# A graph network kernel on one core: the layouts of two more pairs turned by transfers

## The chip, the cores and the metric

The kernel runs on one core of one Trainium2 chip. The metric is the device time of one execution in microseconds (us), of which the median of three runs is given. A profile of one execution shows where the time goes.

## The reference

The input is 64 graphs of 256 nodes with 256 features each, and an adjacency matrix for each graph. Two layers follow one another. The first is a gated graph network of three steps; the second is an attention over neighbours. Each is added to its input and normalised.

```python
def gnn(x, adj, weight, w_ih, w_hh, b_ih, b_hh):
    A = (adj != 0).astype(x.dtype)
    h = x
    for i in range(3):
        m = einsum('bnd,de->bne', h, weight[i])
        aggr = einsum('bst,bsd->btd', A, m)
        h = gru_cell(aggr, h, w_ih, w_hh, b_ih, b_hh)   # r, z: sigmoid; n: tanh
    return h                                             # h = (1 - z) * n + z * h

def gat(h, adj, W, a):
    Wh = h @ W
    e = leaky_relu((Wh @ a1)[:, :, None] + (Wh @ a2)[:, None, :], 0.2)
    attn = softmax(where(adj > 0, e, NEG_INF), axis=2)
    return attn @ Wh

x = layernorm(x + gnn(x, adj, ...))
x = layernorm(x + gat(x, adj, W, a))
```

## The kernel before

Two graphs make a pair, and there are 32 pairs, numbered 0 to 31. One gated step of one pair is a block, written (p, i) for pair p and step i. Blocks run in turns: turn t holds the blocks (t, 0), (t-1, 1) and (t-2, 2), so that three pairs are always under way. The attention of a pair is spread over the two turns after its last step.

The order of all instructions is written out by hand. The function `gates` issues the matrix products of a block (line 468, three pieces of each operand to keep float32 accuracy) and calls `tick` at fixed places in them, 12 ticks in a block. Every other step of the kernel is put on a list with the tick at which it is due (`at`, `after`) and is issued when the clock gets there. Each engine then works through its own instructions in the order of issue. All transfers of the middle of the kernel go out on one queue, that of SyncE (SP).

The work needs two layouts. The products take h with features on the partitions (`hT`). The aggregation over neighbours (`aggregate`, line 439) takes x or h with nodes on the partitions, as two pieces `hi` and `lo` in float32r. So x must be turned once for each pair, and h must be turned back before step 1 and before step 2. There are two ways to do it, and the constant `FROM` tells which pair takes which.

Pairs below `FROM` are turned on TensorE. `to_T` (line 280) turns x with eight 128x128 transposes into PSUM, and an evacuation on ScalarE or VectorE writes `hT`. `from_T` (line 369) turns h with eight transposes before each of the steps 1 and 2; `split` (line 405) and `rest` (line 135) make hi and lo from PSUM. x is loaded (`load_x`) 7 ticks and adj (`load_adj`) 5 ticks after the step before has begun its preparation.

Pairs from `FROM` on are turned by transfers. The transfers that transpose move 16-bit halves, so a float32 value comes out as two planes that must be put together again. `x_turned` (line 347) issues one transposing transfer of x from DRAM into `first`, four copies (line 357) sort the halves into `second`, and `x_joined` writes `hT` with 16-bit copies on ScalarE and VectorE (`put_together`, line 289). For h, `h_turned` issues two transposing transfers from `hT` into `first_h` (line 299) and four copies into `second_h` (line 305); then `join` makes `V` (line 289), `split` makes hi on ScalarE (line 329) and `rest` makes lo on VectorE (line 135). `first` shares the single buffer of x, and `second` and `second_h` share the single buffer of adj, so x and adj of such a pair are loaded only after them, 33 and 34 ticks after the preparation of the block before has begun.

```python
FROM = L + 2
...
nxt = np_ + 1
if nxt < FROM:
    after(7, lambda p=nxt: load_x(p))
elif nxt < NP:
    later = {}
    after(26, lambda p=nxt, d=later: d.update(f=x_turned(p)))
    after(30, lambda d=later: d["f"]())
    after(33, lambda p=nxt: x_joined(p))
    after(33, lambda p=nxt: load_x(p))
after(5 if nxt < FROM else 34, lambda p=nxt: load_adj(p))
```

The ticks at which a block's own steps are due are called its pace. A first step below `FROM` takes the pace `EARLY`; from `FROM` on it takes `FIRST`. Other names that occur below: `ones` (line 380) makes the 0/1 matrix `A` from adj on VectorE; hH, hL and hD are the three pieces of hT (lines 132, 135 and 138, on ScalarE, GpSimd and VectorE), and aH, aL, aD those of the aggregate.

Of the kernel before, what the change touches and what calls it, by code (L numbers as in the profile page):

```python
# [27 lines left out]
def kernel(  # L28
# [39 lines left out]
    L = weight.shape[0]  # L68
# [24 lines left out]
    def after(dt, step):  # L93
        at(clock[0] + dt, step)
# [67 lines left out]
    neg = const.tile([P, 1], F32, name="neg")  # L162

    loaded, loaded_adj = {}, {}
    FROM = L + 2

    def load_x(p):
        if p < NP:
            x_sb = loaded[p] = io.tile([P, G, C, D], F32, tag="x", name=f"x_{p}")
            nc.sync.dma_start(x_sb, x[p * G:(p + 1) * G].rearrange("g (c p) d -> p g c d", p=P))  # L170

    def load_adj(p):
        if p < NP:
            a_sb = loaded_adj[p] = io.tile([P, G, C, N], I32, tag="adj", name=f"adj_{p}")
            nc.sync.dma_start(a_sb, adj[p * G:(p + 1) * G].rearrange("g (c p) n -> p g c n", p=P))
# [100 lines left out]
    def to_T(src, dst, d):  # L276

        pt = bank("pt")
        for k in range(K):
            nc.tensor.transpose(pt[:, k * P:(k + 1) * P], src[:, k // C, k % C, d * P:(d + 1) * P], ident)  # L280
        after(1, lambda: evacuate(dst[:, d, :], pt))
# [25 lines left out]
    def h_turned(p, i, e):  # L307

        s = pairs[p]
        pool, dt = ((late, (16, 19, 22)), (io, (12, 22, 25)))[i]  # L310
        tmp = {}

        def first():
            tmp["a"] = first_of(pool.tile([P, G, C, D], F32, tag=("wh", "x")[i], name=f"first_h{p}_{i}"))
            for d in range(C):
                turn_half(tmp["a"], s.hT, d)

        def second():
            tmp["b"] = second_of(io.tile([P, G, C, D], F32, tag="adj", name=f"second_h{p}_{i}"))
            gather(tmp["b"], tmp["a"])  # L320

        def join(d):
            tmp[d] = work.tile([P, K, P], F32, tag="V", name=f"V{d}_{p}_{i}", bufs=1)
            put_together(tmp[d].rearrange("p k n -> p (k n)"),
                         *(tmp["b"][:, h, :, d * P:(d + 1) * P] for h in (1, 0)), "av" if i == 0 else "va", k=K)

        def split(d):
            s.hi[d] = work.tile([P, K, P], F32R, tag=f"hi{d}", name=f"hi{d}_{p}_{i + 1}", bufs=1)
            nc.scalar.copy(s.hi[d], tmp[d])

        def rest(d):
            s.lo[d] = work.tile([P, K, P], F32R, tag=f"lo{d}", name=f"lo{d}_{p}_{i + 1}", bufs=1)
            lower(nc.vector, s.lo[d], tmp[d], s.hi[d])
        s.hi, s.lo = [None] * C, [None] * C
        at(e + dt[0], first)
        at(e + dt[1], second)
        for d in range(C):
            for n, step in enumerate((join, split, rest)):
                at(e + dt[2] + (2, 4)[i] * d + n, lambda step=step, d=d: step(d))
        s.by_dma = i + 1  # L340
# [31 lines left out]
    def begin(p):  # L372
        s = pairs.setdefault(p, Pair())
        s.hT = work.tile([P, C, GN], F32, tag="hT", name=f"hT_{p}", bufs=4)
# [10 lines left out]
    def front(p, i, t, pace):  # L385
# [7 lines left out]
        def turn(d):  # L393
            s = pairs[p]
            if i == 0:
                if p < FROM:
                    to_T(s.x, s.hT, d)
# [491 lines left out]
    for n, (p, i) in enumerate(blocks):  # L889
        if n + 1 < len(blocks):  # L890
            np_, ni = blocks[n + 1]
            if ni == 0:
                if np_ < FROM:
                    after(1, lambda p=np_: begin(p))
                after(1, lambda p=np_: take_x(p))
                after(2, lambda p=np_: ones(p))
# [4 lines that stand above are left out]
# [4 lines left out]
                    after(33, lambda p=nxt: load_x(p))  # L905
                after(5 if nxt < FROM else 34, lambda p=nxt: load_adj(p))
            front(np_, ni, clock[0], 
                  CLOSE if n and np_ == blocks[n - 1][0] else
                  EARLY if np_ < FROM and not ni else (FIRST, SECOND, THIRD)[ni])
        gates(p, i, (2, 3, 5) if n + 2 >= len(blocks) or blocks[n + 2][0] == p else (2, 5, 9))  # L910
        if i == L - 1:
            if p < NP - len(LAST):
                attention(p, clock[0])
            else:
                attention_last(p, clock[0], LAST[p - NP])
        elif FROM <= p and p + i + 1 < NP:
            h_turned(p, i, clock[0])
# [32 lines left out]
```

## Time and profile before

| | before |
|---|---|
| median of three runs | 2091.16 us (2088.38 to 2096.8) |
| time of the profiled execution | 2091.86 us |
| its span, first to last instruction | 2090.0 us |
| granted TensorE clock | 0.996 |
| packets' bytes moved by DMA | 247.98 MB |

The profile gives each engine's busy time; PE is TensorE's matmuls, PEld its weight loads, DVE is VectorE, ACT ScalarE and POOL GpSimd. A line of a timeline has the start in us, the duration in us, the engine, the kernel's line, the operation, what is written and read, and in brackets how long the engine was idle before it and what ended that. A line of the waits names the engine and line that waited, whom it waited for, the sum in us, how often, and the longest.

### The profile page before, as it was taken

What the parts mean: (1) busy time and instruction counts of PE and PEld (TensorE: products, weight loads), DVE (VectorE), ACT (ScalarE), POOL (GpSimd) and SP (SyncE); (2) the same over time, 40 slices, a digit from 0 to 9 for tenths busy, and PEclk for the clock granted to TensorE, in tenths of its full rate; (3) what the DMA queues carried; (4) which work ended last, traced back from release to release, by engine and by line L of the source; (5) the groups of instructions that cost most, each with busy time, mean ns of one, the idle gap of its engine ahead of it and who ended that gap; (6) DMA issues with size and microseconds to landing.
All of it is one profiled execution on the core that took longest, in us unless ns stands there. A gap on an engine that the chain in (4) does not pass through costs nothing.

```text
span 2090.0 us, 31381 instructions
## 1 busy us (share of the span) xinstructions
PE 2052.3 (98%) x9892; PEld 1726.0 (83%) x9892; DVE 1780.5 (85%) x2886; ACT 1655.3 (79%) x3015; POOL 1604.8 (77%) x1114
## 2 busy tenths in 40 slices
PE   8999999999999999999999999999999999999996
PEld 5788888888888888888888888888888888888885
DVE  5666778898888899888998988998888998988887
ACT  4566787888887888888888887888888888888775
POOL 6777777777877787878777877787878787878763
PEclk9999999999999999999999999999999999999998
DMA  4111235665666665665665666665766665666321
GB/s 131 31 41 41 72 88 114 141 141 117 136 138 135 141 137 121 136 136 137 140 136 124 136 137 137 137 138 123 134 138 139 134 141 123 138 136 137 61 61 61
DMA packets 531621, 247.98 MB, mean 119 GB/s; under 512 B 359616, under 2 KB 523200, under 8 KB 531456
## 3 DMA queue, kind: packets, MB, share of 16 engines
q1 hardware_dynamic: 529664, 244.14, 53.1%
q8 instruction: 79, 1.29, 0.3%
q10 hardware_dynamic: 1616, 1.57, 0.2%
q14 instruction: 86, 0.70, 0.1%
q0 software_dynamic: 176, 0.27, 0.1%
HBM read 69.74 MB, written 33.55 MB: 49 GB/s over the span
## 4 chain that ended last, share of the span: by engine, by line
PE 89%; DVE 3%; ACT 3%; issue 2%; POOL 1%; DMA 1%; SPq 0%; POOLq 0%; ACTq 0%; DVEq 0%
PE pga L468 46%; PE pgb L468 23%; PE pa L439 8%; PE pwh L589 5%; PE po L673 5%; DVE lo L135 1%; PE s L608 1%; PE pt L369 1%; ACT sc L636 1%; DMA rows_hH<-in_L_gnn_w_hh_dram 0%; PE po L796 0%; ACT L636 0%; PE pw L238 0%; ACT n L475 0%; DMA second<-v 0%
## 5 line engine op out<-in xcount | busy, mean ns | idle before, releaser
L494 POOL TENSOR_TENSOR t<-hT,n 128x512 f32<-128x512 f32 x192 | 263.0, 1370 | 191.6 <-ACT n L486 191.3
L500 POOL TENSOR_TENSOR n<-n,r 128x512 f32<-128x512 f32 x192 | 316.5, 1648 | 81.8 <-ACT r L486 42.6
L504 POOL TENSOR_TENSOR n<-n,t 128x512 f32<-128x512 f32 x192 | 282.7, 1472 | 122.7 <-DVE t L477 116.0
L468 PE MATMUL pga<-hH,whhH_whh 128*128 128x512 f32 x1152 | 370.5, 403 | 0.0
L468 PE MATMUL pgb<-hD,whhD_whh 128*128 128x512 f32 x1152 | 356.8, 391 | 1.4 <-DVE hD L138 1.4
L468 PE MATMUL pga<-hL,whhL_whh 128*128 128x512 f32 x1152 | 356.7, 391 | 0.4 <-POOL hL L135 0.4
L495 POOL TENSOR_TENSOR t<-t,z 128x512 f32<-128x512 f32 x192 | 271.4, 1414 | 15.1
L135 POOL TENSOR_TENSOR hL<-hT,hH 128x1024 fp32r<-128x1024 f32 x96 | 255.5, 2661 | 9.0 <-ACT hH L132 9.0
L468 PEld LDWEIGHTS pgb<-hD,whhD_whh 128*128 128x128 f32 x1152 | 216.2, 188 | 49.2 <-DVE hD L138 1.7
L468 PEld LDWEIGHTS pga<-hL,whhL_whh 128*128 128x128 f32 x1152 | 216.2, 188 | 47.8 <-POOL hL L135 0.8
L468 PEld LDWEIGHTS pga<-hH,whhH_whh 128*128 128x128 f32 x1152 | 207.5, 188 | 34.1
L473 ACT ACTIVATE r<-pga 128x512 f32<-128x512 f32 x192 | 114.1, 594 | 109.1 <-PE pga L468 79.6
L439 PE MATMUL pa<-A,lo 128*128 128x256 f32 x768 | 192.5, 283 | 6.1 <-DVE lo L135 6.1
L138 DVE SCALAR_TENSOR_TENSOR hD<-hH,hT 128x1024 fp32r<-128x1024 f32 x96 | 195.7, 2039 | 0.0
L439 PE MATMUL pa<-A,hi 128*128 128x256 f32 x768 | 194.2, 285 | 0.2 <-DVE A L380 0.2
L477 DVE SCALAR_TENSOR_TENSOR r<-pgb,r 128x512 f32<-128x512 f32 x192 | 132.0, 687 | 68.9 <-PE pgb L468 43.4
L486 ACT ACTIVATE n<-n,bi 128x512 f32<-128x512 f32 x192 | 139.1, 724 | 64.0 <-POOL n L504 63.8
L507 DVE TENSOR_TENSOR hT<-t,n 128x512 f32<-128x512 f32 x192 | 185.0, 963 | 0.0
L135 DVE TENSOR_TENSOR aL<-pa,aH 128x512 fp32r<-128x512 f32 x192 | 130.9, 682 | 56.6 <-ACT aH L132 56.5
L473 ACT ACTIVATE t<-pga 128x512 f32<-128x512 f32 x192 | 115.1, 600 | 71.1 <-PE pga L468 66.0
L132 ACT ACTIVATE aH<-pa 128x512 fp32r<-128x512 f32 x192 | 115.8, 604 | 64.0 <-PE pa L439 64.0
L439 PEld LDWEIGHTS pa<-A,lo 128*128 128x128 f32 x768 | 146.4, 191 | 13.8 <-DVE lo L135 7.6
(172 smaller groups left out, 5405.9 us busy)
## 6 DMA issues: line engine op xcount, KB each, us to landing
adj<-in_adj_dram SPq DMA_DIRECT2D x64, 512.0 KB, 3.8
second_h<-first_h SPq DMA_DIRECT2D x204, 128.0 KB, 4.2
x<-in_x_dram SPq DMA_DIRECT2D x32, 512.0 KB, 3.8
xT<-hT SPq DMA_DIRECT2D x32, 512.0 KB, 4.5
vT<-xT SPq DMA_DIRECT2D x32, 512.0 KB, 3.3
second<-v SPq DMA_DIRECT2D x116, 128.0 KB, 3.8
sc<-eT SPq DMA_DIRECT2D x232, 64.0 KB, 2.3
out_dram<-eT SPq DMA_DIRECT2D x29, 512.0 KB, 4.3
```

What stands on the lines that cost most here:

```text
L135: eng.tensor_sub(dst, src, hi.bitcast(F32))
L138: nc.vector.scalar_tensor_tensor(dst, hi.bitcast(F32), 1.0 + U, src, op0=ALU.mult, op1=ALU.subtract)
L439: nc.tensor.matmul(pt[:, g * N:(g + 1) * N], h[:, g * C + c, :], s.A[:, g, c, :], start=(n == 0), stop=(n == len(todo) - 1))
L468: nc.tensor.matmul(pt, w[:, d, o * P:(o + 1) * P], m[:, d, :], start=n in (0, ends + 1), stop=n in (ends, len(todo) - 1))
L473: nc.scalar.activation(dst, a, AF.Copy, scale=1.0 + U)
L477: nc.vector.scalar_tensor_tensor(dst, b, -1.0 / U, dst, op0=ALU.mult, op1=ALU.add)
L486: nc.scalar.activation(dst, dst, func, bias=bias)
L494: nc.gpsimd.tensor_sub(t, h, n)
L495: nc.gpsimd.tensor_mul(t, t, z)
L500: after(2, lambda r=r, n=n: nc.gpsimd.tensor_mul(n, n, r))
L504: after(1, lambda n=n, t=t: nc.gpsimd.tensor_add(n, n, t))
L507: after(lags[2], lambda n=n, t=t, h=h: nc.vector.tensor_add(h, t, n))
```

## The change

`L` is 3, the number of steps. `FROM` goes from 5 to 3, so that pairs 3 and 4 are turned by transfers too. Pairs 0, 1 and 2 stay on TensorE.

```diff
-    FROM = L + 2
+    FROM = L
```

All that depends on `FROM` follows for these two pairs: the transposes and evacuations of `to_T` and `from_T` are not issued; `x_turned`, `x_joined` and `h_turned` are; x and adj are loaded at ticks 33 and 34 instead of 7 and 5; and the first step's pace is `FIRST` instead of `EARLY`.

```python
EARLY = (2, 1, 2, 6, 7, 8), (5, 8, 10)
FIRST = (2, 1, 2, 7, 7, 8), (3, 10, 7)
```

The numbers are the ticks of turn, split, rest, aggregate and the two pieces of the aggregate, and then of hH, hL and hD.

## The prediction

> **What bounds the kernel now.** I read the page first, for the engine that is never idle:
>
> ```profile
> PE 2052.3 (98%) x9892; PEld 1726.0 (83%) x9892; DVE 1780.5 (85%) x2886; ACT 1655.3 (79%) x3015; POOL 1604.8 (77%) x1114
> PE 89%; DVE 3%; ACT 3%; issue 2%; POOL 1%; DMA 1%; SPq 0%; POOLq 0%; ACTq 0%; DVEq 0%
> ```
>
> PE is busy for 98% of the span and holds 89% of the chain that ended last. Second, the longest of PE's own waits:
>
> ```profile
> PE pa L439 <- DVE lo L135: 6.1, 5, 1.2
> ```
>
> Outside the start and the tail this is the only wait that costs PE more than 2 us: five times 1.2 us in 2090. So the middle of the kernel is a stream of matmuls in a fixed order, and what leaves the stream is saved unless something new interrupts it. Third, the timeline of PE around two groups of transposes says what they take from it:
>
> ```profile
> 141.74 0.62 PE L468 MATMUL pgb<-aD,wc2D_wc 128*128 128x512 f32 x2
> 142.19 0.60 PE L280 MATMUL pt<-ident,x 128*128 128x128 f32 x4
> 142.55 0.70 PE L468 MATMUL pga<-hH,whhH_whh 128*128 128x512 f32 x2
> 143.09 0.63 PE L468 MATMUL pga<-hL,whhL_whh 128*128 128x512 f32 x2
> 143.56 0.62 PE L468 MATMUL pgb<-hD,whhD_whh 128*128 128x512 f32 x2
> 144.01 0.60 PE L280 MATMUL pt<-ident,x 128*128 128x128 f32 x4
> ```
>
> Starts matter here, since neighbours overlap. A pair of 128x512 matmuls takes about 0.455 us from start to start. From 142.19 to 144.01 there are 1.82 us, with three such pairs (1.36) and four transposes in them: a group of four costs 0.46 us, 0.115 each, although one lasts 272 ns. Fourth, the table of stretches, cut at the first matmul of each block. Here are blocks (1,2), (2,2), (5,0), (7,0), (4,1), (6,1); the first two columns are the length and PE's busy time:
>
> ```profile
> core 0: us, PE busy (x) PEld busy (x) DVE busy (x) ACT busy (x) POOL busy (x), PEclk, DMA share, GB/s
> 197.20:216.40 19.20, 19.20 (x97) 16.20 (x96) 11.83 (x19) 14.50 (x25) 14.91 (x10) 1.00 0.17 55
> 262.40:280.70 18.30, 18.30 (x90) 15.43 (x89) 16.13 (x32) 14.02 (x24) 16.70 (x12) 1.00 0.46 115
> 280.70:303.90 23.20, 23.20 (x118) 19.60 (x117) 16.23 (x27) 18.81 (x39) 15.60 (x14) 1.00 0.13 46
> 408.20:430.50 22.30, 22.30 (x109) 18.83 (x108) 17.91 (x34) 19.73 (x41) 16.40 (x14) 1.00 0.34 95
> 303.90:326.60 22.70, 22.70 (x113) 19.23 (x112) 17.48 (x28) 17.34 (x31) 16.18 (x10) 1.00 0.58 140
> 430.50:452.30 21.80, 21.80 (x105) 18.47 (x104) 20.09 (x27) 18.76 (x33) 16.73 (x10) 1.00 0.63 132
> ```
>
> The rows come in couples: the same kind of block with eight transposes, then without. The differences are 0.9 us each, PE is full in both, and ACT, DVE and DMA carry more in the second and still do not stop it. This is the change, already run on later pairs.
>
> **What the Trainium skill says.** "Perfetto Trace Analysis", section "Identifying the Most-Contended Engine", says that pipelined matmuls make busy time a poor measure of PE; agreed, which is why I price by starts: 272 ns by its record against 0.115 us. "TensorE: Matmul & The Clock Gate", section "Part 4: PE-mode transpose", puts a transpose in a kernel at about 275 ns; the record agrees (272), the cost to a full PE does not. "DMA: Bandwidth & Descriptors", section "DMA Transpose (X-bar)", says that such a transfer moves 2-byte types only and lands in SBUF; that is why the code turns 16-bit halves and joins them afterwards. "SBUF — State Buffer", section "SBUF: two separate sides", says that a DVE operation with two SBUF inputs and a GpSimd one that reads SBUF exclude each other for a whole instruction. The trace agrees, on one pair of instructions, in blocks (9,1) and (10,1):
>
> ```profile
> 628.00 2.93 DVE L135 TENSOR_TENSOR lo<-V,hi 128x512 fp32r<-128x512 f32 x1
> 628.00 2.38 POOL L135 TENSOR_TENSOR hL<-hT,hH 128x1024 fp32r<-128x1024 f32 x1
> 630.99 0.39 PE L439 MATMUL pa<-A,lo 128*128 128x256 f32 x1 [1.22 <-DVE lo L135]
> ...
> 691.85 0.68 DVE L135 TENSOR_TENSOR lo<-V,hi 128x512 fp32r<-128x512 f32 x1
> 691.85 2.94 POOL L135 TENSOR_TENSOR hL<-hT,hH 128x1024 fp32r<-128x1024 f32 x1
> ```
>
> Both start together. When DVE goes first nothing is lost; when POOL goes first, lo takes 2.93 us instead of 0.68 and PE waits. That is all five waits above; the block is 23.27 us long instead of 21.79, so a lost draw costs 1.48 us. It is lost 5 times in 25 turns.
>
> **The change part by part.**
> Removed from PE: per pair 8 transposes of x (L280) and 8 of h for each of two layers (L369), 24; 48 for two pairs, in six blocks of eight. By starts 48 x 0.115 = 5.5 us. By blocks: x in (0,2) and (1,2), 19.24 to 18.30, 0.94 each; h in (4,0) and (5,0), 23.21 to 22.29, 0.92 each; h in (4,1), 22.73 to 21.79, 0.94; h in (5,1), 22.75 to 21.79, 0.96. Sum 5.62. I take 5.6 us off; PE is full on both sides, so it lies on the path.
> ACT and DVE: per pair ACT loses 5 evacuations of 0.58 (2.9) and gains 2 joins of 0.77, 4 V copies of 0.77 and 4 hi of 0.61 (7.1): +4.2. DVE loses 5 of 0.68 (3.4) and gains 2 of about 0.7, 4 V of 0.87 and 4 lo of 0.72 (7.8): +4.4. Taken at nothing: blocks (7,0) and (6,1) above hold this load at ACT 19.73 and DVE 20.09 with PE full. The cover ends where a block has more than PE's length of it; without cover the cost would be at most the sum for two pairs, about 9 us.
> Order of the join of pair 3. It comes before aH and aL of (0,2). aD ended at 137.7 and PE takes it at 141.74. Two joins on ACT (1.4) and two on DVE (1.3) add at most 2.7: ready by 140.4. Nothing.
> SP. Per pair one DRAM transpose (4.6 us to landing), four copies into second (3.1), and twice two transposes (3.7) and four copies (4.2): 17 issues, 34 in all, on the one queue that also carries x, adj, xT, vT and the attention's eT. x and adj of pairs 3 and 4 move behind first, second and, for adj, the join. For pair 3 the join ends near 135 us; adj then needs 0.4 to issue and 3.8 to land, 139.2; ones(3) ran on DVE at 140.45. Margin about 1 us there and 8 us at PE (the aggregate starts at 148.58). No attention uses the queue yet. In the later turns the same chain leaves x and adj 4.4 and 2.9 us early (x issued 696.47, hi at 704.73; adj issued 700.94, A at 707.49). Between 0 and one landing (3.8 us) per pair, 0 to 8 in all; I take 0. A gain is excluded, since PE does not wait for x or adj there.
> Pace. Pair 3 and 4 take FIRST for EARLY: the aggregates one tick later, hL two ticks later, hD three earlier. PE's count is unchanged and the later turns run it; nothing.
> New draws. The blocks (4,1) and (5,1) get the lo and hL that start together: 2 x 5/25 x 1.48 = +0.6. The other 25 are drawn anew.
>
> Sum for the profiled execution: 2090.0 - 5.6 + 0.6 = 2085.0 of span, plus the 1.86 around it: 2086.9 against its 2091.86. Its time lies 0.7 above the median shown, so the median goes from 2091.16 to 2086.2, -0.24%. A measurement of this kernel can tell about 0.5% (10.5 us) from no change, and the three runs spread over 8.4 us, so by that measure this is "the same".
>
> **Rivals.**
> A, all draws lost. The transfers shift the turn so that POOL goes first each time: 27 lost for 5, 22 x 1.48 = 32.6, less 5.6: 2118. For it: the two start within 10 ns. Against: it won 20 of 25, and the late turns lost none. It ends slower than before from 4 more losses, slower by 0.5% from 11 more. One or two more is likely, eleven is not.
> B, all draws won. 5 x 1.48 = 7.4 on top: 2078. For it: the last seven turns are clean. It takes four fewer losses to pass 0.5%.
> C, late adj. SP's queue in turns 3 and 4 delivers late and DVE stands at ones, with the gates' evacuations queued behind it: +3.8 per pair, 2093. Against: the same chain is early in a fuller queue.
> D, hidden transposes. If another engine set these blocks, nothing would change: 2091. Against: the couples of blocks above, 0.9 us apart.
> E, full price. If a transpose cost its 272 ns, 13 us: 2078. Against: the starts.
>
> **How the numbers follow.** The forecast, with losses within three of five: 0.81, 2082 to 2091. B, with four or more fewer: 0.06. A: 0.05, of which 0.02 beyond 0.5%. C 0.05, a fifth of it beyond 0.5% if it hits more turns; D 0.02; E 0.01. Leaving out the far ends gives 2080.5 to 2091.5. Faster by over 0.5%: B and E, 0.07. Slower: 0.03. Same: 0.90.
>
> **What would show it.** Blocks (0,2) and (1,2) at 18.3, (4,0) and (5,0) at 22.3, (4,1) and (5,1) at 21.8, and L280 at 24 and L369 at 72 of hT instead of 40 and 104. Wrong would be: a PE wait on A, hi or aL between 120 and 410 us; those blocks still 0.9 longer; or a count of 2.9 us long lo far from five.

## The result and the profile after

The changed kernel takes 2080.35 us (2078.74 to 2080.64, four runs) against 2093.18 (2088.38 to 2096.8) of the kernel before in the same comparison: a ratio of 0.9934, 95% interval 0.9919 to 0.9949. That is 12.8 us or 0.66% faster, clear of noise, and 2.6 times the forecast of 5.0 us. 2080.35 lies just below the range given.

The head of the page and the chain that ended last:

```profile
span 2078.6 us, 31369 instructions
PE 2048.2 (99%) x9844; PEld 1724.7 (83%) x9844; DVE 1787.8 (86%) x2896; ACT 1659.6 (80%) x3025; POOL 1616.4 (78%) x1114
PE 96%; DVE 1%; POOL 1%; ACT 1%; DMA 0%; issue 0%; POOLq 0%; ACTq 0%; SPq 0%; DVEq 0%
```

PE has 48 matmuls fewer, ACT and DVE ten instructions more each, and the chain is now PE for 96% of the span instead of 89%. The transposes that are left, by line (duration least, median, most):

```profile
L280 PE MATMUL pt<-ident,x x24: 270/347/448, 6.0 to 89.1; 128*128 128x128 f32 x24
L369 PE MATMUL pt<-ident,hT x72: 270/272/421, 70.8 to 2000.3; 128*128 128x128 f32 x72
```

The six blocks that lost transposes, in the table of stretches: (0,2), (1,2), (4,0), (5,0), (4,1), (5,1). Length first, then PE's busy time:

```profile
142.00:160.30 18.30, 18.30 (x90) 15.45 (x89) 13.54 (x19) 11.57 (x20) 16.88 (x11) 1.00 0.51 141
198.70:217.00 18.30, 18.30 (x89) 15.43 (x88) 15.13 (x22) 14.16 (x25) 16.88 (x11) 1.00 0.79 167
217.00:239.30 22.30, 22.30 (x110) 18.84 (x109) 19.21 (x33) 17.79 (x37) 16.36 (x14) 1.00 0.16 47
280.30:302.60 22.30, 22.30 (x109) 18.83 (x108) 18.15 (x35) 20.01 (x42) 16.94 (x14) 1.00 0.33 95
302.60:324.40 21.80, 21.80 (x106) 18.47 (x104) 20.09 (x27) 18.76 (x33) 16.74 (x10) 1.00 0.55 130
365.00:386.70 21.70, 21.70 (x105) 18.43 (x104) 20.00 (x27) 18.65 (x33) 16.65 (x10) 1.00 0.58 130
```

They are as long as their later counterparts, and PE is full in each. From block start to block start they are 5.7 us shorter in sum than before. PE's own waits, the four longest (sum, times, longest):

```profile
PE pt L280 <- DMA x<-in_x_dram: 6.0, 1, 6.0
PE pt L784 <- ACT sc L772: 4.4, 7, 1.4
PE pt L369 <- DVE vT L707: 3.1, 1, 3.1
PE pw L247 <- ACT gwT L229: 2.3, 1, 2.3
```

Every wait of PE of more than 0.1 us now lies in the first 70 us or in the tail. The line of `pa` waiting for `lo` (6.1 us, five times) is gone altogether: all 27 draws between lo and hL were won. Block (9,1), one of the five that had lost:

```profile
624.84 0.68 DVE L135 TENSOR_TENSOR lo<-V,hi 128x512 fp32r<-128x512 f32 x1
624.84 2.94 POOL L135 TENSOR_TENSOR hL<-hT,hH 128x1024 fp32r<-128x1024 f32 x1
```

The two profiles differ by 11.4 us of span. Block by block: -5.7 in the six blocks, five times -1.48 (-7.4) in the blocks of the lost draws, -0.5 in (24,0), where one `pwh` no longer waits, -0.5 in the tail, and +2.5 in the start-up, whose instructions are unchanged: block (0,0) starts at 23.0 instead of 21.8 and is 32.4 long instead of 31.1. The start differs that way between other kernels below too, so it is not put down to the change.

### The profile page after: what moved, and what is told of

Read it like the earlier page. It is cut to its first block, busy times and chain, and to the rows that moved or that the text cites. A ratio compares the mean times of both kernels' runs of the same rounds, so it can differ in the third digit from the quotient of the medians.

```text
span 2078.6 us, 31369 instructions
## 1 busy us (share of the span) xinstructions
PE 2048.2 (99%) x9844; PEld 1724.7 (83%) x9844; DVE 1787.8 (86%) x2896; ACT 1659.6 (80%) x3025; POOL 1616.4 (78%) x1114
## 4 chain that ended last, share of the span: by engine, by line
PE 96%; DVE 1%; POOL 1%; ACT 1%; DMA 0%; issue 0%; POOLq 0%; ACTq 0%; SPq 0%; DVEq 0%
PE pga L468 50%; PE pgb L468 25%; PE pa L439 9%; PE pwh L589 5%; PE po L673 5%; PE s L608 1%; PE pt L369 1%; PE pw L238 0%; DMA rows_hH<-in_L_gnn_w_hh_dram 0%; PE pwh L733 0%; PE po L796 0%; POOL wc2L_wc L149 0%; DVE cut L135 0%; PE pw L219 0%; POOL t L494 0%
## 5 line engine op out<-in xcount | busy, mean ns | idle before, releaser
L135 POOL TENSOR_TENSOR hL<-hT,hH 128x1024 fp32r<-128x1024 f32 x96 | 260.5, 2714 | 9.1 <-ACT hH L132 9.0
L138 DVE SCALAR_TENSOR_TENSOR hD<-hH,hT 128x1024 fp32r<-128x1024 f32 x96 | 203.2, 2117 | 0.0
L507 DVE TENSOR_TENSOR hT<-t,n 128x512 f32<-128x512 f32 x192 | 191.1, 995 | 0.0
L486 ACT ACTIVATE z<-z,b_sum 128x512 f32<-128x512 f32 x192 | 140.7, 733 | 19.6 <-DVE z L477 19.1
```

The source lines that it names most:

```text
L135: eng.tensor_sub(dst, src, hi.bitcast(F32))
L138: nc.vector.scalar_tensor_tensor(dst, hi.bitcast(F32), 1.0 + U, src, op0=ALU.mult, op1=ALU.subtract)
L486: nc.scalar.activation(dst, dst, func, bias=bias)
L507: after(lags[2], lambda n=n, t=t, h=h: nc.vector.tensor_add(h, t, n))
```

## The experiments

Kernels of one group ran beside each other and beside the kernel before. The kernel before differs between groups: medians 2089.5, 2092.6, 2087.2, 2088.3, 2087.5 in groups 1 to 5. Only comparisons inside a group are used, or profiles. A draw is the start of lo on VectorE and of hL on GpSimd within a few ns of each other. It comes once for each pair p whose h goes by transfers, while its step 2 is prepared, in block (p+1, 1); it is lost when GpSimd goes first. "Lost" counts the lo of over 2.9 us in the one profile of a kernel; the runs that were not profiled can only be judged by their times.

### Is it the draws? Making each side win

First form, group 1. A new tile of 4 bytes per partition, and a tiny operation on it that delays one of the two rivals. GpSimd is delayed by

```diff
+    pad = const.tile([P, 1], F32, name="pad")
 def h_lower():
+    if i == 2:
+        nc.gpsimd.memset(pad, 0.0)
     lower(nc.gpsimd, flat(s.hc[1]), flat(s.hT), flat(s.hc[0]))
```

> The kernel before, with one GpSimd operation on 128x1 elements put ahead of every hL of step 2 (the first piece of the pair that starts together with lo). It leaves all else in its order. Theory 'draws': the part of the gain that the forecast missed is the lost draws between lo on VectorE and hL on GpSimd; here GpSimd always comes second, so no lo takes 2.9 us, the five PE waits of 1.2 us are gone, and the time is about 7.4 us below before on the same chip, 0.35%. Rival 'elsewhere': the missed part comes from the earlier turns or the transfers; then this kernel stays within 2 us of before.

and VectorE by

```diff
 def rest(d):
+    if i == 1 and d == 1:
+        nc.vector.memset(pad, 0.0)
     lower(nc.vector, s.lo[d], tmp[d], s.hi[d])
```

> The kernel before, with one VectorE operation on 128x1 elements put ahead of the second lo of step 2 of each pair turned by transfers (25 of them), so that VectorE comes second. Theory 'draws': GpSimd wins all 25, every one of these lo takes about 2.9 us, each turn is 1.4 to 1.5 us longer, and the kernel is 20 x 1.48 = 30 us slower than before (some 2121). If a lost draw were covered by something else in most turns, it would stay within 5 us of before.

Measured: 2116.2 (2115.8 to 2116.8) with GpSimd late and 2143.3 (2143.1 to 2145.0) with VectorE late, before 2089.5. Both are far above what was expected. The counts came out as meant, 0 and 25 lost, and the two differ by 27.1 us, 1.07 for each block with a lost draw and not 1.48; but the blocks from (0,1) on, but for the last few, had become 0.25 to 0.4 us longer, also where neither operation occurs. Something other than the operation was at work. A tile of 32 bytes instead of 4 (group 2):

> The kernel before with one GpSimd operation of 128x1 elements ahead of every hL of step 2, its target now a tile of 32 bytes per partition instead of 4 bytes. Theory 'address': the 4-byte tile shifted every later tile and made each 512-column matmul 6 ns longer, which was the 33 us of the first form; with 32 bytes the blocks are as long as before (18.30 for (2,2)), no draw is lost, and the time is 2083 to 2086, 3 to 7 us below before. Rival: the operation itself lengthens the turns; then the time is near 2116 again.

2117.0, 0 lost: the same. So the size of the tile was not it. The third form (group 3) writes to `warm`, a scratch tile that was there already, and moves no address:

> The kernel before with one GpSimd operation of 128x1 elements ahead of every hL of step 2, its target now an existing scratch tile, so that no address moves. Theory 'draws' and 'address' together: blocks keep their lengths (18.30 for (2,2)), all 25 draws are won, and the time is that of before less its lost draws: 2082 to 2085.5. If the operation itself made every block longer, it is 2116 again.

> The kernel before with one VectorE operation of 128x1 elements ahead of the second lo of step 2, its target an existing scratch tile. Theory 'draws': all 25 draws are lost, each at 1.0 to 1.5 us, and the kernel is 25 to 37 us above the one whose draws are all won: 2110 to 2121. Rival 'covered': a lost draw costs nothing when it happens in each turn; then it stays at before.

Now 2086.1 (2084.6 to 2087.1), none lost, and 2121.6 (2119.5 to 2124.4), 24 of 25 lost; before 2087.2. Both medians lie 0.6 us above the upper bounds that were expected, and the kernel before loses little in this group: without its losses it is only 1.1 us faster. With the operation ahead of hL, lo goes first:

```profile
441.30 0.10 POOL L426 MEMSET warm<- 128x1 f32 x1
441.32 0.68 DVE L135 TENSOR_TENSOR lo<-V,hi 128x512 fp32r<-128x512 f32 x1
441.35 2.90 POOL L135 TENSOR_TENSOR hL<-hT,hH 128x1024 fp32r<-128x1024 f32 x1
```

PE's waits with the operation ahead of lo:

```profile
PE pa L441 <- DVE lo L135: 29.4, 24, 1.2
```

The difference of 35.4 us over 24 draws is 1.48 each, the price read from the profile of before. A stretch of the two engines in the same kernel shows the loser:

```profile
440.79 2.92 DVE L135 TENSOR_TENSOR lo<-V,hi 128x512 fp32r<-128x512 f32 x1
440.78 2.39 POOL L135 TENSOR_TENSOR hL<-hT,hH 128x1024 fp32r<-128x1024 f32 x1
```

So the mechanism and its price are shown. The kernel before with the operation ahead of hL ran at 2084.6 to 2087.1, a spread about as large as that of the start-up, whose end, the start of block (1,0), lies 52.8 to 55.7 us after the first instruction in the profiles here. In the comparison of the result the kernel before was at 2088.4 to 2096.8. If the band without losses was the same there, it lost at least one draw in each run and several in most. None of these four runs was profiled; the profile of before, of another run at 2091.86, has five lost.

What had made the first forms slow was tried alone: the tile, filled once in the start-up, and nothing else (group 4).

```diff
+    pad = const.tile([P, 8], F32, name="pad")
+    nc.gpsimd.memset(pad, 0.0)
```

> The kernel before with one more 32-byte tile allocated among the constants and filled once in the start-up, otherwise unused; every later tile lies 32 bytes further on. Theory 'address': each 512-column matmul goes from 227 to 233 ns, the block (2,2) from 18.30 to 18.69, and the time is 33 us above before less or more its draws: about 2117 to 2124. Rival: the operations did it, not the addresses: 2084 to 2092.

2117.4, one run, none lost. The block (2,2) is 18.69 us instead of 18.30, and the commonest matmul, in the groups of instructions of this kernel (line 470 is line 468 of before), takes 396 ns by its record instead of 391:

```profile
L470 PE MATMUL pga<-hL,whhL_whh 128*128 128x512 f32 x1152 | 362.6, 396 | 0.0
```

### Which part of the change wins the draws?

x alone and h alone (group 2), with the changed kernel again. The condition of `h_turned` is set apart from `FROM`; for h alone `FROM` stays at 5:

```diff
-        elif FROM <= p and p + i + 1 < NP:
+        elif L + 2 <= p and p + i + 1 < NP:     # x alone (FROM = L)
+        elif L <= p and p + i + 1 < NP:         # h alone (FROM = L + 2)
```

> x of pairs 3 and 4 by transfers, h of these pairs turned on TensorE as before. 16 transposes go, in blocks (0,2) and (1,2), 0.95 us each: -1.9 us against before with equal draws. The profile is to show both blocks at 18.3 and (4,0), (5,0), (4,1), (5,1) as before. Theory 'phase': lost draws anywhere from 0 to 8. If the transfers of x are what wins the draws, none is lost and the time is 2082 to 2085.

> h of pairs 3 and 4 by transfers, x of these pairs turned on TensorE as before, with the early loads of x and adj and the pace EARLY. 32 transposes go, in blocks (4,0), (5,0), (4,1), (5,1): -3.75 us against before with equal draws. Theory 'phase': lost draws anywhere from 0 to 8 of 27. If the transfers of h are what wins the draws, none is lost and the time is 2080 to 2083.

> The changed kernel once more. Theory 'chance': each execution draws anew and the changed kernel was lucky; then some of these runs lose draws and the times spread from 2078 to some 2088, with the median near 2084. Theory 'phase': the changed kernel wins its draws in every execution; then all runs lie between 2078 and 2081, and the profile has no lo of 2.9 us.

| group 2 | median us | range | transposes taken out, by the blocks | lost |
|---|---|---|---|---|
| before | 2092.55 | 2087.96 to 2097.31 | | |
| x alone | 2092.95 | 2088.75 to 2098.19 | -1.9 | 3 of 25 |
| h alone | 2081.03 | 2080.40 to 2083.42 | -3.75 | 0 of 27 |
| the change | 2079.57 | 2077.88 to 2080.19 | -5.7 | 0 of 27 |

x saves its two blocks, 0.95 each, as the profile shows, but draws go on being lost and the time does not move. With h by transfers no draw is lost in the profile, and the kernel is 11.5 us faster for 3.75 us of PE work. The change loses none again, and its five runs lie within 2.3 us, so its winning was not the chance of one execution. The waits of PE with x alone:

```profile
PE pa L439 <- DVE lo L135: 3.7, 3, 1.2
```

One pair instead of two: pair 4 alone with x and h (group 1), h of pair 3 alone (group 3), h of pair 4 alone (group 4).

```diff
-    FROM = L
+    FROM = L + 1                                               # pair 4, x and h
-        elif FROM <= p and p + i + 1 < NP:
+        elif (FROM <= p or p == 3) and p + i + 1 < NP:         # h of pair 3 (FROM = L + 2); p == 4 likewise
```

> FROM at 4: pair 4 alone is turned by transfers besides the later ones. By the blocks, half the PE gain: 3 blocks of eight transposes, -2.8 us against before, +2.8 against the change, if the draws stay as in either. Theory 'phase': the count of lost draws is newly set by each edit; any count from 0 to 8, so 2083 (none) to 2095 (eight). If the draws are won because both pairs have gone, five are lost: about 2088.

> h of pair 3 alone by transfers, all else as before: 16 transposes go, from (4,0) and (4,1), -1.85 us. Theory 'history': the earliest turn whose h goes by transfers sets the phase; pair 3 alone then wins all draws as both pairs did: 2082 to 2085. If both pairs are needed, it stays with about three to five lost draws: 2087 to 2091.

> h of pair 4 alone by transfers, all else as before: 16 transposes go, from (5,0) and (5,1), -1.9 us. If one pair next to pair 5 is enough to win the draws: 2082.5 to 2085, narrow. If it takes both pairs, or if it is by chance of the phase: a spread of 2082.5 to 2091.

Pair 4 whole: 2087.5 (2081.5 to 2092.0), before 2089.5; none lost in the profile, which was its fastest run. h of pair 3: 2085.8 (2082.1 to 2087.5), between the two bands that were expected, before 2087.2; one lost. h of pair 4: 2086.4 (2083.8 to 2091.6), before 2088.3; one lost. These save 2.0, 1.4 and 1.9, about their PE work (2.8, 1.85, 1.9), and keep spreads of 5 to 11 us: the draws are no better than before. Of the versions tried, only those with h of both pairs win nearly all.

### Why are they won? Three causes tried

The bank of PSUM. The changed kernel takes 12 banks fewer from the rotation of eight, so all later products go to other banks. They were put back unused (group 1):

```diff
 if p < FROM:
     to_T(s.x, s.hT, d)
+elif p < L + 2:
+    bank("pt")
...
+if by_dma and p < L + 2:
+    for d in range(C):
+        at(t + pace[0][0] + d, lambda: bank("pt"))
```

> The changed kernel, with one PSUM bank taken from the rotation, unused, where each group of four transposes of pairs 3 and 4 stood (12 in all). The instructions and their order are those of the changed kernel; only the bank that each later product goes to is again the one of the kernel before. Theory 'banks': which bank the products use sets the fine timing that decides the draws; then about five draws are lost again and the time is 5 to 8 us above the changed kernel (about 2087). Theory 'phase': the banks do not matter; no lost draw or one, 2079 to 2082.

2078.9 (2078.2 to 2080.7), 0 of 27 lost: not the banks, as far as one profile and four runs tell. The place in the program (group 3): eight small operations each on ScalarE and VectorE in the start-up of the kernel before, as many as h by transfers adds.

```diff
+    for _ in range(8):
+        nc.scalar.copy(warm, half)
+        nc.vector.memset(b_sum, 0.0)
```

> The kernel before with eight small ScalarE and eight small VectorE operations in the start-up, on existing scratch tiles; as many as h of pairs 3 and 4 by transfers adds to each of the two. Nothing after the start-up moves, except that each later instruction stands eight places further in its engine's program. Theory 'place': where an instruction stands in the program sets the fine timing; then the draws are won as with h by transfers, 2082 to 2086. Theory 'history': the turns 3 to 6 set the phase that later turns keep; then about as many draws are lost as before and the time is within 2 us of before.

2087.2 (2085.2 to 2090.3) against 2087.2 of before: no effect, although the one profile shows no loss; this group's kernel before lost few draws itself, so the run tells less than was hoped. A phase that turns hand on (group 4): one loss is forced in the changed kernel, with the VectorE operation on `warm` at pair 6 alone.

```diff
 def rest(d):
+    if p == 6 and i == 1 and d == 1:
+        nc.vector.memset(warm[:, :1], 0.0)
```

> The changed kernel with one VectorE operation of 128x1 elements ahead of the second lo of step 2 of pair 6 alone, so that one draw is lost, in block (7,1). Theory 'history': the turns carry a phase from one to the next, and a loss shifts it; then further draws are lost in later turns, 2 to 8 in all, and the time is 3 to 10 us above the changed kernel. Theory 'immune': only the forced loss, +1.5 us: 2079.5 to 2082.5.

2083.6 (2079.1 to 2084.4): the median lies above the upper bound of "immune" and at the lower end of "history". The profile, of a run of 2082.5, shows 1 of 27 lost, the forced one:

```profile
PE pa L441 <- DVE lo L135: 1.2, 1, 1.2
```

In the same group the kernel with h of pair 2 as well, below, took 2080.3; it lacks 1.9 us of PE work that this one has, and 1.4 us are left between them, one draw. So a loss did not bring others after it in that profile, and that sum agrees; the slower runs were not profiled.

### One pair further

h of pair 2 by transfers as well, x of pair 2 still on TensorE:

```diff
-        elif FROM <= p and p + i + 1 < NP:
+        elif L - 1 <= p and p + i + 1 < NP:
```

> The change, and h of pair 2 by transfers as well (its x stays on TensorE). 16 more transposes go, from the blocks before (2,1) and (2,2), which are (1,1)'s turn mates (3,0) and (3,1): -1.9 us against the change if the draws are won: 2075.8 to 2079, median about 2077.5. If the phase is lost with it: 2080 to 2086.

2080.3 (2079.1 to 2080.6), none lost in the profile, above the 2077.5 expected; its tail was 1.5 us and its block (5,0) 0.4 us longer than those of the changed kernel in the result's profile. So it was put beside the change on one chip (group 5):

> The changed kernel again, beside the next one on the same chip. No draw lost: a range of at most 3 us over its runs, 5.6 us plus the lost draws of before below before.

> The change with h of pair 2 by transfers as well: 1.9 us below the changed kernel on the same chip by the blocks, with no draw lost in either.

The change: 2080.4 (2078.9 to 2082.2), 0 of 27 lost, ratio to before 0.9966 (0.9954 to 0.9978); its range of 3.3 us is a little wider than the 3 expected. With h of pair 2: 2078.3, five of six runs 2077.6 to 2079.7 and one 2086.3. It is 2.1 us faster. The two blocks (3,0) and (3,1) give 1.9 of that (18.28 and 21.79 us instead of 19.23 and 22.75). But its profile also has a start-up 2.1 us shorter than that of the change beside it, and one lost draw in 28, 1.5 us; so the agreement with 1.9 is in part luck, and the winning is not absolute. This is the fastest version here. Its ratio to before, 0.9963 (0.9948 to 0.9977), overlaps that of the change.

## Why the prediction was wrong

The bound and the price of the transposes held. 5.6 us were forecast and 5.7 measured, in the six blocks named, with PE full in each. A price by record durations (rival E, 13 us) would have come nearer the measured 12.8, for a wrong reason: the blocks show 0.95 for eight transposes, not 2.2.

The covers held too. ACT at 20.0 and DVE at 20.1 us did not stop PE. The two joins of pair 3 delayed aD of (0,2) by 2.7 us, the size stated: it ended 1.0 us after the first matmul of (0,2) instead of 1.7 before it, and PE takes it 2.3 after. That size was in part luck. ScalarE's joins did not hold VectorE up. VectorE's own two took 1.8 us, and the addition behind them (hT, line 507) took 1.78 instead of 0.68: it started while GpSimd was at line 495 and ended 0.55 us after it. A of pairs 3 and 4 ran with no idle time before it, so SP's queue was in time, and rival C fell.

The step that failed is "New draws". It put the lost draws at 5 in 25, added two draws at that rate, and treated the rest as drawn anew, as if by chance: 5.4 lost. None was. That term was +0.6 against the profile of before and should have been -7.4: 8.0 us. In the profile the span came to 2078.6 instead of the 2085.0 forecast: 8.0 less by this term, 1.0 less by (24,0) and the tail, and 2.5 more by the start-up. Rival B, all draws won, was the case that came; its 2078 is close to the measured 2080, but it was given 6 in 100 and left outside the range. The frequency in one profile was taken for a rate of chance that no edit elsewhere would move. With h of pairs 3 and 4 by transfers, none of the 135 draws in the five profiles of the change, its bank form and h alone was lost. In the three other profiles with h of both, one draw in 82 was lost without being forced. By its times the kernel before lost some in most of its runs. Even in the profile of before the five losses do not look like independent draws: they lie in blocks (9,1), (12,1), (15,1), (19,1) and (23,1), three or four turns apart, with none before or after. With x alone they lie in (15,1), (23,1) and (25,1). What makes such a spacing was not found.

The base was weak as well. The three runs shown spread over 8.4 us, which a handful of lost draws at 1.48 us each would make; the range should have reached down to a kernel without any.

What stays open is why h of both pairs wins the draws in later turns, whose instructions are the same. Putting the banks back brought no loss, and in the profile one forced loss did not bring others. The place in the program is unlikely, not excluded. How much of a gain the change shows therefore depends on the kernel before: 12.8 us where by its times it loses many, 7.2 in group 5 where it loses few, and 5.7 of it are the transposes taken out.

## What to carry to other kernels

Price a matmul that leaves a full TensorE by the distance between starts in a block with and without it. When two operations of which one holds up the other, here lo on VectorE and hL on GpSimd, start within a few ns of each other, price both outcomes for all occurrences and let the range hold both ends: the count in one profile is no rate. Better still, take the tie out: with a GpSimd operation of 0.1 us ahead of hL none was lost in the profile. That was worth 1.1 us beside a kernel that lost few; beside one that loses many it was not tried.

## What the runs showed that was not expected

One more tile among the constants, which moves every later tile, made the kernel 29 us slower than the kernel before beside it (2117.4 in one run against 2088.3): each 512-column matmul then starts 234 ns after the one before it instead of 227, by the median of the starts, and a block of the same 88 matmuls is 0.39 us longer. A tile of 4 bytes and one of 32, each with the GpSimd operation, did the same, and that operation without a new tile did not. The tile and one filling of it in the start-up are all that changed, so where the tiles lie in SBUF is worth 1.4% here, more than the change. The traces show no addresses; which tile and which alignment matter was not tried.
